# Wide attention taken apart between the first narrow heads, and two experts' products in one block

## The chip, the cores and the metric

The kernel runs on one core of a Trainium2 chip. The core has five engines, each with its own queue of instructions that it works off in order: TensorE (matrix products, PE in the profile; PEld is its loading of weights), VectorE (DVE), ScalarE (ACT), GpSimd (POOL) and SyncE (SP, which here only issues DMAs). They wait for one another by semaphores. The metric is the device time of the whole program in microseconds (us). The kernel before took 855.35 us, the median of 3 runs (854.04 to 857.73).

## The reference

The input x is 8 sequences (batches) of 512 tokens of width 128. Two layers follow, each between layer norms and with a residual:

```python
x = x + layernorm(attention(layernorm(x)))      # one head of width 128, rotary, causal
x = x + layernorm(ffn_layer(layernorm(x)))
```

`attention` is one causal head: q, k, v are products of x with 128x128 matrices, q and k are turned by rotary angles, then softmax(q k) v and an output product.

`ffn_layer` works on the same tokens, here as 8 batches of 512:

```python
h = rmsnorm(x, g1); c = h @ w_down                      # 128 -> 64
q, k, v = rope(c @ wq), rope(c @ wk), c @ wv            # 16 heads of width 4
x = x + (softmax(causal(q k / 2)) v) @ w_up             # 64 -> 128
t = rmsnorm(x, g2); probs = softmax(t @ router_w)       # 8 experts
gate = the two largest probs, divided by their sum, 0 elsewhere
y = sum over e of gate[e] * ((silu(t @ w1[e]) * (t @ w3[e])) @ w2[e])   # 128 -> 256 -> 128
return x + y
```

All experts are worked out for all tokens, and the gate is 0 for six of the eight.

## The kernel before, in words

Tokens lie on the 128 partitions, four tiles (NT = 4) of 128 tokens a batch. The first layer is called the wide attention, the 16 heads of width 4 the narrow heads.

*The wide attention* is a generator, `wide_attention`. Its loop runs over b from 0 to 9: in one turn of the loop it projects and scores batch b, turns and weighs the probabilities of batch b-1, and adds up batch b-2. `project` multiplies a product in PSUM by the rotary table into `two` (VectorE) and adds the halves (GpSimd). `scores` makes two PSUM tiles of scores; for each of the four row tiles VectorE takes the negated maximum and ScalarE the exponential. `turn_probs` turns a row tile of probabilities on TensorE (a product with the identity) and copies it to SBUF. `weigh` multiplies by the values and scales by the sums. `norm_result`, `add_result`, `add` and `norm_sum` do the layer norm of the result, the residual, and the scales `h_scale` for what follows. A `yield` is a point at which other work can be put between.

*A narrow unit* is one of 32: batch u.b, group u.g of four heads. For each unit `rowwise` makes scores by rows (tiles `sm`) of which VectorE takes the maxima into `nm` (`highest`, line 608); `lower` splits these on GpSimd in three bfloat16 parts, `turn_m` turns them (`m3T`) and SyncE puts them by DMA as further rows under q; then `columnwise` makes the same scores by columns (`sT`), less the maximum, ScalarE takes the exponential into `pk` (`weights`, line 672), and `weigh` (line 679) multiplies by the values into `po`.

`ffn_front(b)` makes q, k and v of a batch's narrow heads: four scaled tiles `hs` on GpSimd, their turn `hT`, the products `pqk` and `pvs`, the rotary part, the split in three, and six DMAs of GpSimd's queue that store q and k to DRAM (line 545). `load_rows(b)` brings them back by four DMAs, also of GpSimd's queue (line 553), as the rows that the units read. `ffn_back(b)` divides by the sums, turns (`onT`), makes `pu`, the norm, `tT` and the router's logits; `route` works out the gates of two batches at a time and puts them on the list `ready`.

*The experts.* `hidden_pieces` makes one piece at a time: two products of 128x512 (`ph`, line 851) into one wide PSUM tile, the silu on ScalarE (line 859) and a product on VectorE (line 860). Two pieces make an expert's hidden layer. `answer` makes an expert's sixteen second products (`py`, line 875), and VectorE adds them to `h_all` with the gate (line 884).

*The order.* It is written out by hand: `manual_schedule` keeps the instructions of each engine in the order in which the program issues them. `period(n)` issues the columns of unit n, the rows of unit n+2 and the last weighing of unit n-1; at its yields, `aside` puts in a step of a front, a back or a later task. Periods -2 and -1 have rows only. Before, they are issued between the last loops of the wide attention, and periods 0 to 32 follow. From the first batches with gates on, a period also has two experts: four pieces at its end with the scores of row tiles 1 and 0 between them, and the two `answer` calls of the expert pair before, spread over the row part of the next period.

*The buffers.* A pool called wide has three PSUM tiles of two banks, in turn for `sm`, `sT`, `ph`, `py`, `pqk`, `sc` and `pq`. A pool called bank has two tiles of one bank while the wide attention runs, and afterwards one, beside one for `po`. SBUF tiles `pk` have five buffers, hidden tiles four.

Of the kernel before, what the change touches and what calls it, by code (L numbers as in the profile page):

```python
# [22 lines left out]
def kernel(  # L23
# [181 lines left out]
    h_all = keep.tile([P, B * NT, D], F32, name="h_all")  # L205
    tT_all = keep.tile([P, B, T], F32, name="tT_all")
    gate_all = keep.tile([P, B * NT, E], F32, name="gate_all")
# [63 lines left out]
    def stats_x(batches):  # L271
        st = ln_stats(x_all, batches[0] * NT, "x", len(batches) * NT)
        for i, b in enumerate(batches):
            x_stats[b] = st[0][:, i * NT : (i + 1) * NT, :], st[1][:, i * NT : (i + 1) * NT]

    class Wide:
# [7 lines left out]
        def norm(self):  # L284
            b = self.b
            mv, rstd = x_stats.pop(b)
            shift = minus_product(mv[:, :, 0], rstd, "shift_x", f"shift_x_{b}")
# [15 lines left out]
        def project(self, i):  # L303
            b = self.b
            pq = wide(f"pq_{b}_{i}")
            for s in range(2):
                nc.tensor.matmul(pq[:, s, :], wqk[:, i, s, :], self.xnT, start=True, stop=True)
            two = deep.tile([P, 2, T], F32, tag="pk", name=f"two_{b}_{i}", bufs=5)
            nc.vector.tensor_tensor(two, pq, ropea, ALU.mult)
            r = work.tile([P, T], F32, tag=f"roped{i}", name=f"roped_{b}_{i}", bufs=1)  # L310
            nc.gpsimd.tensor_tensor(r, two[:, 0, :], two[:, 1, :], ALU.add)
            self.roped.append(r)
# [39 lines left out]

        def turn_probs(self, t):
            b = self.b
            n, at = (t + 1) * P, t * (t + 1) // 2 * P
            if t == 0:
                self.pT = work.tile([P, 10 * P], F32, tag="pT", name=f"pT_{b}", bufs=1)
            ps = bank(f"pT_ps_{b}_{t}")
            for j in range(t + 1):
                nc.tensor.transpose(  # L360
                    ps[:, j * P : (j + 1) * P], self.probs[t][:, j * P : (j + 1) * P], ident
                )
            if t < 2:
                nc.vector.tensor_copy(self.pT[:, at : at + n], ps[:, :n])
            else:
                nc.scalar.copy(self.pT[:, at : at + n], ps[:, :n])

# [364 lines left out]
    def normed(b):  # L732
# [23 lines left out]
        ps = transposed(ts, f"tT_ps_{b}")  # L756
        nc.scalar.activation(tT_all[:, b, :], ps, AF.Copy, scale=g2c)
        yield
        pl = bank(f"pl_{b}")
        for t in range(NT):  # L760
            nc.tensor.matmul(
                pl[:, t * E : (t + 1) * E],
                tT_all[:, b, t * P : (t + 1) * P],
                wr,
# [76 lines left out]
    def hidden_pieces():  # L841
        while True:
# [3 lines left out]
            for e in range(E):  # L846
                hid = []
                for c in range(FC):
                    ph = wide(f"ph_{b}_{e}_{c}")
                    for i, w in enumerate((w1s, w3s)):  # L850
                        nc.tensor.matmul(  # L851
                            ph[:, i, :],
                            w[:, e, c * P : (c + 1) * P],
                            tT_all[:, b, :],
                            start=True,
# [70 lines left out]

    turns, partly = [0], []
    N = B * NG
    units = [Unit(n) for n in range(N)]

    def period(n):
# [25 lines left out]
        if nxt:  # L957
            nxt.turn_m()
        answer()
        yield  # L960
# [44 lines left out]
    def wide_attention():  # L1005
# [6 lines left out]
        for b in range(B + 2):  # L1012
            yield b
            u = batches[b] if b < B else None
            nxt = batches[b + 1] if b + 1 < B else None
            v = batches[b - 1] if 0 <= b - 1 < B else None
            w = batches[b - 2] if 0 <= b - 2 < B else None
            if nxt:
                nxt.norm()
            if w:  # L1020
                w.norm_result()
            if u:
                u.project(0)
            if v:
                v.turn_probs(0)
                v.turn_probs(1)
            if u:
                u.project(1)
            yield b
            if v:  # L1030
                v.turn_probs(2)
                v.turn_probs(3)
            if w:
                w.add_result()
                w.add()
            if u:
                u.values()
            if w:
                w.norm_sum()
            yield b  # L1040
# [9 lines left out]
            if u:  # L1050
                u.scores(1)
            yield b

    def front_and_rows(b):
# [3 lines left out]

    with tc.manual_schedule():
        steps = wide_attention()  # L1060
        setup = [prepare(), fill()]
        first = [front_and_rows(0)]
        then = [period(-2), period(-1)]
        fronts.append(front_and_rows(1))
        banks(ctx, wide=3)
        with ExitStack() as stage:
            banks(stage, bank=2)
            for b in steps:
                if b > B:
                    break  # L1070
                if b < 3:
                    step(setup)
                elif b < 6:
                    step(first)
                elif b < 7:
                    step(fronts)
                else:
                    step(fronts)
                    step(then)
            while step(then):  # L1080
                step(fronts)
# [83 lines left out]
```

## Time and profile before

| what | value |
|---|---|
| median of 3 runs | 855.35 us |
| profiled execution, whole | 860.74 us |
| its span, first to last instruction | 859.0 us |
| mean granted clock of TensorE | 0.954 |
| busy: TensorE, VectorE, ScalarE, GpSimd | 761.6, 482.8, 385.2, 310.6 us |
| projections (`pq`) of batches 3 to 7 begin at | 54.1, 73.4, 85.8, 107.2, 125.1 us |
| first scores by row (`sm`) | 124.0 us |
| first product of an expert (`ph`) | about 303 us |
| copies of `m3T`, one a period, in periods 12 and 30 | 292.8 and 670.9 us |

The profile is of one execution. Its page gives the busy time of each engine over the span, 40 equal slices of the span with the busy share in tenths, groups of instructions by line, and what ended the idle time before them. "Granted clock" is the share of TensorE's full clock. A line of a timeline reads: start, length, engine, source line, operation, output<-inputs, shape, how many in a row, and in brackets the idle time before it with what ended it. A line of the windows reads: stretch, length, then busy time (number of instructions) of PE, PEld, DVE, ACT and POOL, the granted clock, the DMA share and GB/s.

### The profile page before, as it was taken

What the parts mean: (1) busy time and instruction counts of PE and PEld (TensorE: products, weight loads), DVE (VectorE), ACT (ScalarE), POOL (GpSimd) and SP (SyncE); (2) the same over time, 40 slices, a digit from 0 to 9 for tenths busy, and PEclk for the clock granted to TensorE, in tenths of its full rate; (3) what the DMA queues carried; (4) which work ended last, traced back from release to release, by engine and by line L of the source; (5) the groups of instructions that cost most, each with busy time, mean ns of one, the idle gap of its engine ahead of it and who ended that gap; (6) DMA issues with size and microseconds to landing.
All of it is one profiled execution on the core that took longest, in us unless ns stands there. A gap on an engine that the chain in (4) does not pass through costs nothing. (4 is left out here: it accounts for less than half of the span.)

```text
span 859.0 us, 15100 instructions
## 1 busy us (share of the span) xinstructions
PE 761.6 (89%) x5886; PEld 437.1 (51%) x5886; DVE 482.8 (56%) x1111; ACT 385.2 (45%) x574; POOL 310.6 (36%) x637
## 2 busy tenths in 40 slices
PE   3988687499998899999999999999999988889995
PEld 1555445244544455555545555555555555466663
DVE  2565565648566855556675655567565334364554
ACT  2464343247555644554455454554454652222221
POOL 5575868526465740425042513240114104010001
PEclk9999798559899999999999999999999999999998
DMA  9000121204022400220012002200000000000000
GB/s 281 14 6 0 56 56 56 57 2 106 11 68 48 105 10 2 56 57 14 2 57 56 14 2 56 58 14 2 2 1 14 1 2 12 1 0 13 1 13 13
DMA packets 24131, 28.74 MB, mean 33 GB/s; under 512 B 6332, under 2 KB 19292, under 8 KB 24060
## 3 DMA queue, kind: packets, MB, share of 16 engines
q0 software_dynamic: 6944, 19.03, 8.6%
q1 hardware_dynamic: 15820, 7.84, 3.3%
q8 instruction: 46, 0.75, 0.4%
q10 hardware_dynamic: 1296, 0.92, 0.4%
q14 instruction: 25, 0.20, 0.1%
HBM read 15.73 MB, written 11.53 MB: 32 GB/s over the span
## 5 line engine op out<-in xcount | busy, mean ns | idle before, releaser
L672 ACT ACTIVATE pk<-sT 128x1024 f32<-128x1024 f32 x160 | 161.9, 1024 | 113.9 <-PE sT L576 113.1
L608 DVE TENSOR_REDUCE nm<-sm 128x2 f32<-128x1024 f32 (+2 forms) x192 | 195.4, 1041 | 25.8 <-PE sm L576 23.4
L860 DVE TENSOR_TENSOR hid<-hid,ph 128x512 f32<-128x512 f32 x128 | 87.7, 686 | 155.8 <-ACT hid L859 155.2
L859 ACT ACTIVATE hid<-ph 128x512 f32<-128x512 f32 x128 | 76.0, 597 | 210.0 <-PE ph L851 172.4
L851 PE MATMUL ph<-tT_all,w1s 128*128 128x512 f32 x256 | 139.0, 625 | 6.2 <-DVE hid L860 6.2
L875 PE MATMUL py<-w2s,hid 128*128 128x128 f32 x1024 | 128.6, 279 | 4.2 <-DVE nm L608 1.3
L851 PE MATMUL ph<-tT_all,w3s 128*128 128x512 f32 x256 | 131.6, 596 | 0.0
L875 PEld LDWEIGHTS py<-w2s,hid 128*128 128x128 f32 x1024 | 120.7, 192 | 21.1 <-issue 9.8
L884 DVE SCALAR_TENSOR_TENSOR h_all<-py,gate_all,h_all 128x128 f32<-128x128 f32 x256 | 72.0, 343 | 63.8 <-PE py L875 63.7
L679 PE MATMUL po<-pk,vpad 128*32 128x512 f32 (+3 forms) x1024 | 99.2, 463 | 0.0
L217 POOL TENSOR_TENSOR root_o<-ve_o,half 128x4 f32<-128x4 f32 x8 | 8.3, 1037 | 220.6 <-DVE ve_o L234 220.6
L593 PE MATMUL sm<-k_rows,q_rows 36*128 36x256 bf16 (+3 forms) x512 | 72.2, 317 | 9.7 <-DVE nm L608 6.6
L851 PEld LDWEIGHTS ph<-tT_all,w3s 128*128 128x128 f32 x256 | 49.0, 192 | 62.1 <-issue 62.1
L593 PEld LDWEIGHTS <-q_rows 36*128 36x128 bf16 x512 | 23.5, 95 | 97.6 <-issue 94.0
L649 PE MATMUL sT<-q_rows,k_rows 39*128 39x384 bf16 (+3 forms) x512 | 64.8, 310 | 9.3 <-ACT pk L672 4.3
L431 POOL CAST m<-nm 128x16 bf16<-128x16 f32 x32 | 6.4, 199 | 176.6 <-DVE nm L608 176.1
L851 PEld LDWEIGHTS ph<-tT_all,w1s 128*128 128x128 f32 x256 | 42.4, 191 | 50.4 <-issue 17.7
L576 PE MATMUL sm<-ident_bf,mask_q 64*128 64x64 bf16 (+1 forms) x768 | 49.6, 205 | 0.0
L576 PEld LDWEIGHTS <-mask_q 64*128 64x128 bf16 x768 | 39.5, 100 | 13.6 <-issue 2.1
L576 PE MATMUL sT<-ident_bf,mask_k 64*128 64x128 bf16 (+1 forms) x640 | 43.2, 210 | 0.0
L576 PEld LDWEIGHTS <-mask_k 64*128 64x128 bf16 x640 | 31.0, 98 | 13.5 <-issue 2.0
L649 PEld LDWEIGHTS <-k_rows 39*128 39x128 bf16 x512 | 23.2, 96 | 23.1 <-issue 20.3
(170 smaller groups left out, 942.0 us busy)
## 6 DMA issues: line engine op xcount, KB each, us to landing
q_dram<-thirds POOLq DMA_DIRECT2D x24, 192.0 KB, 3.1
k_dram<-thirds POOLq DMA_DIRECT2D x24, 192.0 KB, 3.6
q_rows<-q_dram POOLq DMA_DIRECT2D x16, 288.0 KB, 5.3
k_rows<-k_dram POOLq DMA_DIRECT2D x16, 288.0 KB, 6.4
q_rows<-m3T SPq DMA_DIRECT2D x192, 2.0 KB
x_all<-in_L_attn_x_dram SPq DMA_DIRECT2D x8, 256.0 KB
out_dram<-y SPq DMA_DIRECT2D x8, 256.0 KB
w1s<-in_L_ffn_w_dram SPq DMA_DIRECT2D x2, 512.0 KB
```

Of the source, the lines that this page charges most:

```text
L217: nc.gpsimd.tensor_tensor(y, x, half[:, :n], ALU.pow)
L576: nc.tensor.matmul(out[:, :, h * HR : (h + 1) * HR], which[at, h, :], ident_bf[at, at].unsqueeze(1).to_broadcast([HR, out.shape[1], HR]), ...
L593: nc.tensor.matmul(sc[:, i, c * n : (c + 1) * n], self.q[at, 2 * self.g + pair, t * P : n], self.k[at, 2 * self.g + pair, :n], start=(c == 0),
L608: nc.vector.tensor_reduce(self.nm[:, :, pairs[0] : pairs[0] + w, t], sc[:, :, : w * n].rearrange("p i (c n) -> p i c n", n=n), AX.X, ALU.m ...
L649: nc.tensor.matmul(sc[:, i, c : c + n], self.k[at, 2 * self.g + pair, j * P : (j + 1) * P], self.q[at, 2 * self.g + pair, j * P :], start= ...
L672: nc.scalar.activation(p[:, :, :c], sc[:, :, :c], AF.Exp, scale=HD**-0.5)
L679: nc.tensor.matmul(po[h * HP : (h + 1) * HP, j * P :], vpads[self.g][:, j, h, :], self.p[j, h // 2][:, h % 2, :], start=(self.g == 0 and j ...
L851: nc.tensor.matmul(ph[:, i, :], w[:, e, c * P : (c + 1) * P], tT_all[:, b, :], start=True, stop=True,)
L859: nc.scalar.activation(hid[c], ph[:, 0, :], AF.Silu)
L860: nc.vector.tensor_tensor(hid[c], hid[c], ph[:, 1, :], ALU.mult)
L875: nc.tensor.matmul(py[:, t * P : (t + 1) * P], hid[c][:, t * P : (t + 1) * P], w2s[:, e, c, :], start=(c == 0), stop=(c == FC - 1),)
L884: nc.vector.scalar_tensor_tensor(h_all[:, n, :], py[:, t * P : (t + 1) * P], gate_all[:, n, e : e + 1], h_all[:, n, :], ALU.mult, ALU.add,)
```

## The change

It has two parts. In the first, the wide attention's loop is cut into seven pieces a turn instead of five, in a new order, and only its first five turns run alone: as soon as batch 0's narrow rows have been asked for, the periods begin, and the rest of the loop is issued piece by piece at their yields (at each in periods -2 and -1, at every second later). A period that needs a later batch's sum first issues the pieces up to it. The pool bank has one tile from period -2 on. Three row tiles of probabilities are turned together into a wide tile, and all copies of them are ScalarE's; `two` has one buffer of its own; the shift of x is worked out with its statistics; `tT` has six tiles instead of one for each batch.

In the second, a period with experts ends with one block: the rows of tiles 1 and 0, both `answer` calls of the period before, and then the four pieces. The row part has no `answer` any more.

```diff
     def stats_x(batches):
...
-            x_stats[b] = st[0][:, i * NT : (i + 1) * NT, :], st[1][:, i * NT : (i + 1) * NT]
+            rstd = st[1][:, i * NT : (i + 1) * NT]
+            mean = st[0][:, i * NT : (i + 1) * NT, 0]
+            x_stats[b] = minus_product(mean, rstd, "shift_x", f"shift_x_{b}"), rstd
...
-            two = deep.tile([P, 2, T], F32, tag="pk", name=f"two_{b}_{i}", bufs=5)
+            two = work.tile([P, 2, T], F32, tag="two", name=f"two_{b}_{i}", bufs=1)
...
-        def turn_probs(self, t):
+        def turn_probs(self, *tiles):
...
+            parts = [(t, j) for t in tiles for j in range(t + 1)]
+            n, at = len(parts) * P, tiles[0] * (tiles[0] + 1) // 2 * P
+            if len(parts) > 4:
+                ps = wide(f"pT_ps_{b}_{tiles[0]}").rearrange("p a n -> p (a n)")
+            else:
+                ps = bank(f"pT_ps_{b}_{tiles[0]}")
...
-            if t < 2:
-                nc.vector.tensor_copy(self.pT[:, at : at + n], ps[:, :n])
-            else:
-                nc.scalar.copy(self.pT[:, at : at + n], ps[:, :n])
+            nc.scalar.copy(self.pT[:, at : at + n], ps[:, :n])
...
-        nc.scalar.activation(tT_all[:, b, :], ps, AF.Copy, scale=g2c)
+        tT = tTs[b] = work.tile([P, T], F32, tag="tT", name=f"tT_{b}", bufs=6)
+        nc.scalar.activation(tT, ps, AF.Copy, scale=g2c)
...
         if u and u.g == 1 and u.b + 2 < B:
+            while u.b + 2 not in done:
+                next(wides)
             fronts.append(ffn_front(u.b + 2))
...
         if nxt:
             nxt.turn_m()
-        answer()
         yield
...
         both(2, C, u, ((0, 1),))
-        answer()
-        yield
-        mixed = bool(ready) or bool(partly)
-        if mixed:
+        yield
+        if (ready or answers) and B - 1 in done:
...
+            both(1, AC, None, None)
+            both(0, AC, None, None)
+            if v:
+                v.lower()
+                v.values()
+            answer()
+            answer()
             for i in range(2 * FC):
-                partly[:] = [b for b in (next(hidden),) if b is not None]
-                if i < 2:
-                    both(1 - i, AC, None, None)
-                if i == 2 and v:
-                    v.lower()
-                    v.values()
+                next(hidden)
                 step(later)
...
         for b in range(B + 2):
...
+            if u:
+                u.project(0)
+            if w:
+                w.norm_result()
+            yield b
+            if v:
+                v.turn_probs(0, 1, 2)
+            yield b
+            if u:
+                u.project(1)
+            if w:
+                w.add_result()
+            yield b
+            if v:
+                v.turn_probs(3)
+            if w:
+                w.add()
             if nxt:
                 nxt.norm()
...
             yield b
             if u:
                 u.values()
+            yield b
             if w:
                 w.norm_sum()
-            yield b
             if v:
                 v.weigh()
-            if b + 2 < B:
-                stats_x([b + 2])
+            yield b
             if nxt:
                 nxt.turn()
...
                 u.scores(1)
+            if b + 2 < B:
+                stats_x([b + 2])
             yield b
+            done.append(b - 2)
...
+    with tc.manual_schedule(), ExitStack() as stage:
+        banks(stage, bank=2)
+        for b in wides:
+            if b < 3:
+                step(setup)
+            else:
+                step(first) or step(fronts)
+            if b == 5 and not first:
+                break
     banks(ctx, bank=1, po=1)
     with tc.manual_schedule():
-        for n in range(N + 1):
-            for _ in period(n):
-                next(steps, None)
+        for n in range(-2, N + 1):
+            for i, _ in enumerate(period(n)):
+                if n < 0 or i % 2:
+                    next(wides, None)
                 aside()
         while ready or answers or fronts or backs or later:
-            if next(hidden) is not None:
+            more = next(hidden)
+            if more is not None:
                 aside()
                 next(hidden)
-            if len(answers) > 1 or not ready:
+            if len(answers) > 1 or more is None:
                 answer()
             aside()
```

More of the change, by code (lines that the diff above doesn't have):

```diff
@@ L205 @@
     h_all = keep.tile([P, B * NT, D], F32, name="h_all")
-    tT_all = keep.tile([P, B, T], F32, name="tT_all")
+    tTs = {}
     gate_all = keep.tile([P, B * NT, E], F32, name="gate_all")
@@ L285, in norm @@
             b = self.b
-            mv, rstd = x_stats.pop(b)
-            shift = minus_product(mv[:, :, 0], rstd, "shift_x", f"shift_x_{b}")
+            shift, rstd = x_stats.pop(b)
             self.xn = work.tile([P, NT, D], F32, tag="xn", name=f"xn_{b}")
@@ L351, in scores @@
                 self.probs.append(p)
-        def turn_probs(self, t):
+        def turn_probs(self, *tiles):
             b = self.b
-            n, at = (t + 1) * P, t * (t + 1) // 2 * P
-            if t == 0:
+            if 0 in tiles:
                 self.pT = work.tile([P, 10 * P], F32, tag="pT", name=f"pT_{b}", bufs=1)
-            ps = bank(f"pT_ps_{b}_{t}")
-            for j in range(t + 1):
+            parts = [(t, j) for t in tiles for j in range(t + 1)]
[4 more added lines that the diff above has]
+                ps = bank(f"pT_ps_{b}_{tiles[0]}")
+            for i, (t, j) in enumerate(parts):
                 nc.tensor.transpose(
-                    ps[:, j * P : (j + 1) * P], self.probs[t][:, j * P : (j + 1) * P], ident
+                    ps[:, i * P : (i + 1) * P], self.probs[t][:, j * P : (j + 1) * P], ident
                 )
-            if t < 2:
-                nc.vector.tensor_copy(self.pT[:, at : at + n], ps[:, :n])
-            else:
-                nc.scalar.copy(self.pT[:, at : at + n], ps[:, :n])
+            nc.scalar.copy(self.pT[:, at : at + n], ps[:, :n])
         def weigh(self):
@@ L762, in normed @@
                 pl[:, t * E : (t + 1) * E],
-                tT_all[:, b, t * P : (t + 1) * P],
+                tT[:, t * P : (t + 1) * P],
                 wr,
@@ L853, in hidden_pieces @@
                             w[:, e, c * P : (c + 1) * P],
-                            tT_all[:, b, :],
+                            tTs[b],
                             start=True,
@@ L925, in aside @@
         step(a) or step(b) or step(later)
-    turns, partly = [0], []
+    turns, done = [0], []
     N = B * NG
@@ L1017, in wide_attention @@
             w = batches[b - 2] if 0 <= b - 2 < B else None
+            if u:
[15 more added lines that the diff above has]
+                w.add()
             if nxt:
                 nxt.norm()
[L1020 to L1028, printed above, removed]
-            yield b
[L1030 to L1035, printed above, removed]
+            yield b
             if u:
                 u.values()
+            yield b
             if w:
                 w.norm_sum()
-            yield b
             if v:
                 v.weigh()
-            if b + 2 < B:
-                stats_x([b + 2])
+            yield b
             if nxt:
@@ L1057, in front_and_rows @@
         load_rows(b)
[L1059 to L1081, printed above, removed]
+    wides = wide_attention()
+    setup = [prepare(), fill()]
+    first = [front_and_rows(0)]
+    fronts.append(front_and_rows(1))
+    banks(ctx, wide=3)
+    with tc.manual_schedule(), ExitStack() as stage:
[7 more added lines that the diff above has]
+                break
     banks(ctx, bank=1, po=1)
     with tc.manual_schedule():
-        for n in range(N + 1):
-            for _ in period(n):
-                next(steps, None)
+        for n in range(-2, N + 1):
+            for i, _ in enumerate(period(n)):
+                if n < 0 or i % 2:
+                    next(wides, None)
                 aside()
         while ready or answers or fronts or backs or later:
-            if next(hidden) is not None:
+            more = next(hidden)
+            if more is not None:
                 aside()
                 next(hidden)
-            if len(answers) > 1 or not ready:
+            if len(answers) > 1 or more is None:
                 answer()
```

## The prediction

> **What bounds the kernel now.** I read the 40 slices first, then the windows, then the timeline.
>
> ```profile
> PE   3988687499998899999999999999999988889995
> PEclk9999798559899999999999999999999999999998
> ```
>
> A slice is 21.5 us. TensorE is the bound from slice 9 on, nearly full and at full clock. The loose stretch is slices 2 to 8 (the wide attention, then the first narrow heads): gaps, and a clock down to half. Windows (us; busy per engine; granted clock):
>
> ```profile
> 152.00:165.00 13.00, 4.59 (x50) 2.59 (x49) 11.36 (x29) 0.26 (x1) 7.73 (x17) 0.62 0.38 92
> 172.00:180.00 8.00, 7.75 (x68) 2.71 (x65) 3.66 (x4) 3.25 (x4) 3.02 (x11) 0.50 0.01 2
> 180.00:189.20 9.20, 8.94 (x71) 4.89 (x68) 3.98 (x5) 4.71 (x6) 1.01 (x5) 0.50 0.01 1
> ...
> 525.60:544.43 18.83, 18.47 (x160) 9.91 (x159) 10.73 (x19) 10.11 (x14) 5.02 (x13) 1.00 0.22 65
> 194.49:202.16 7.67, 7.10 (x111) 3.41 (x109) 6.10 (x7) 5.31 (x6) 6.63 (x14) 1.00 0.52 145
> ```
>
> From 152 to 165 VectorE's reductions (11.36 of 13) hold TensorE at 4.59. Next to last is a period with two experts: only 0.36 of 18.83 us idle. Last is one without: 0.57 of 7.67.
>
> **Part 1: wide batches in pieces.** The instruction counts hardly change: TensorE, ScalarE the same, VectorE 16 fewer (copies of turned probabilities, 345 ns each, 5.5 us, hidden: VectorE is 56% busy). So all turns on order. Batches 0 and 1 should stay (batch 2's projection starts at 41.6). From batch 2 to 4 the wide attention still runs alone, in a new order: VectorE does batch 2's statistics for the batch two back after the first rotary product, and ScalarE's four scalings (1.65) stand before the second copy of probabilities. One such batch, from its projection: reductions and exponentials of the batch before to 2.1, statistics of x 1.4, rotary product 1.2 (4.7), statistics 1.4 and `ve` (6.3), root 1.04 and shift 0.46 (7.8), scalings 1.65 (9.5), copy 0.6 (10.1), the ten weighting products 2.3, four turns 0.5, scores 2.6: 15.6, where 41.6 to 54.1 was 12.5. Batch 3, with the narrow front, by the same sum 21 (now 19.3).
>
> Batch 4 is where a DMA is moved. On GpSimd's queue:
>
> ```profile
> 94.99 0.63 POOL L545 DMA_DIRECT2D k_dram<-thirds  x1
> 100.32 1.27 POOL L407 TENSOR_TENSOR x_all<-x_all,h_all 128x512 f32<-128x512 f32 x1
> 105.98 1.49 POOL L553 DMA_DIRECT2D q_rows<-q_dram  x2 [0.41 <-issue]
> 107.45 1.32 POOL L553 DMA_DIRECT2D k_rows<-k_dram  x2
> ```
>
> Today the row loads are issued 10.4 us after the last store's issue; the stores land in 3.6, so nothing waits. In the new order only x_all's sum (1.27) stands between: the loads wait about 1.7 us on GpSimd. Queued behind them are batch 1's scaled rows, batch 2's `h_scale`, and the next shift; for the rows waits hT's transpose, which TensorE has before batch 5's projection. GpSimd's sum from the first rotary addition: additions 2.5, root and shift 1.5, thirds 1.8, six stores 3.9, sum 1.3, wait 1.7, four loads 2.8, rows 1.8, `h_scale` 2.3 = 19.6. It starts at 6.8 (after root_x and the first thirds), so hT comes at about 26.4, while scores end near 17.5: an 8.5 us stall. Batch 4 takes 28 for today's 12.4, and batch 5 starts at 41.6 + 15.6 + 21 + 28 = 106, today 85.8.
>
> Now the pieces pay. Periods -2 and -1 carry batches 5 and 6, each paced by the three wide PSUM buffers and the single bank rather than by TensorE (15.6 and 13.8 us of its work): following reductions (1.24, 0.93, 1.22, 0.68), rotary products 1.2 and statistics through VectorE's queue I get 19.4 and 18.2. Periods 0 to 5: TensorE work today at full clock 6.5, 10.0, 7.1, 7.1, 9.0, 7.7 = 47.4; the rest of the wide work 14.3; 1 us of gaps in each (today 0.57 to 1.66): 68. Periods 6 to 11 stay at 63.7, their half-clock stretch included.
>
> The clock. The Trainium skill ("TensorE: Matmul & The Clock Gate", Part 1) says that a busy window of about 3.4 us restores full clock. The rows disagree: from 172 to 189 TensorE is 97% busy at 0.50. By the page the 8.5 us stall costs some 2 us after it; if periods -2 and -1 stay at half as they do today (155 to 189), the cost is up to 17. I take 9: the neighbours are the same narrow products, but wide float32 ones now lie among them.
>
> Block starts at 106 + 19.4 + 18.2 + 9 + 68 + 63.7 = 284 instead of 293: **8.5 us gained**.
>
> **Part 2: first and second products in one block.** Around 541.33, the end of a block now (PE, ACT, DVE):
>
> ```profile
> 543.95 2.05 PE L875 MATMUL py<-w2s,hid 128*128 128x128 f32 x16
> 546.16 0.38 PE L649 MATMUL sT<-q_rows,k_rows 39*128 39x512 bf16 x2
> ...
> 542.21 1.28 ACT L672 ACT_TABLE_LOAD   x1 [0.17 <-PE sT L576]
> 543.51 1.02 ACT L672 ACTIVATE pk<-sT 128x1024 f32<-128x1024 f32 x1
> ...
> 542.67 2.35 DVE L608 TENSOR_REDUCE nm<-sm 128x2 f32<-128x1024 f32 x2
> ```
>
> After a block ScalarE loads its table and ends the first exponential 3.1 us later; VectorE, finishing the last product, frees its first score buffer at 2.6. TensorE's own work there lasts only 2.4, and `py` (1.98) covers the difference; the second `py` covers the next. Without them: the next scores wait 0.25 for the reduction, columns 0.3 for the exponential, then 0.2, 0.15 and 0.2 as three buffers pass between reduction (0.93) and exponential (1.02), and the first `py` 0.2 for the fourth exponential: about 1.2 of gaps for 0.36, **+0.8** in a plain period. Where a back's `onT` copy stands behind that exponential, `pu` waits 1.0 more: +1.3. Where hT is turned, m3T waits for its copy (0.83 today) and tT for m3T's: +0.7. The period with neither: +0.6. Mean 0.85. In the block itself (scores 0.8, two `py` 4.0, four `ph` 7.5) every buffer is back in time: a `ph` gives its own back 1.4 us after it ends, and the next user comes 3.8 later. Sixteen periods x 0.85 = 13.6, and three at the end without scores by row, 0.7 each: **15.7 lost**. Bounds: 0, if the gaps now seen (0.73 a period) only change place, and 24, if all 1.28 of the table load show in 19 periods.
>
> **Small edits.** One `two` buffer: the second product waits for the first addition (1.27), covered by 1.4 us of statistics; uncovered 1.3 a batch. Six tT tiles for eight: the seventh is wanted after batch 0's experts are done; were it not, the router would be late. Turned probabilities in a wide buffer: its ScalarE copy of 768 lies between the 512 one (0.59) and the exponential of 1024 (1.02); taken 0.8, counted above. The tail's order of products is the same: 0.
>
> **Sum.** -8.5 + 15.7 = +7, on the profiled execution (span 859.0, 860.7 with what lies around it, 5.4 above the median). I carry the difference to the median: 855.35 + 7 = **862**.
>
> **Rivals.**
> (a) *Pieces at TensorE's pace*, ends faster: if the GpSimd wait hides and the clock holds, from 106 there are 145 us of TensorE work and some 12 of gaps: block at 263, -30; with +15.7, 841. For it: slices 7 and 8 are that empty. Against: GpSimd is over half busy there and gates hT. It decides once the early gain passes 20.
> (b) *The block is hidden anyway*: gaps stay at 0.73 a period; -8.5 gives 847. For it: three engines with slack; against: periods without experts already idle as much without a table load.
> (c) *Half clock stays*: the stall is followed by 35 us more at 0.50, about +15, and gaps for the single bank: 880. For it: 172 to 189; against: slices 9 to 11 recover.
> (d) *It moves nothing*: the pieces only take up the gaps of one another, and so does the block: 855.
>
> **Numbers.** Forecast 0.42 (853 to 872; 0.10 of it within 0.5%, 0.32 above), (a) 0.16, (b) 0.14 (0.12 faster, 0.02 same), (c) 0.20, (d) 0.08 same. A change under 0.5% (4.3 us) can't be told from none. Faster 0.28, same 0.20, slower 0.52. The range cuts off the ends of (a) and (c): 840 to 884.
>
> **What would show it.** Right: batch 5's projection beyond 100; before it a gap of 5 us or more at hT, GpSimd in its loads; the first `ph` 5 to 15 us earlier than 303; plain periods with experts near 19.6, `sT` waiting for `pk` and `sm` for `nm`. Wrong: no gap at hT, full clock throughout 100 to 200, or periods at 18.8 or less.

## The result, and where the profile shows it

The changed kernel has a median of 892.1 us (4 runs, 884.60 to 903.87), the kernel before, beside it, one of 856.54 (4 runs, 854.04 to 857.78). Two of the changed kernel's runs, 899.36 and 903.87, are over 1.5% longer than its shortest and had a lower mean clock (0.920 and 0.915, for 0.934), so its ratio, like every ratio below, leaves such runs out: the other two, at 884.6 and 884.8, are **1.033 times as long** as the kernel before, 95% interval 1.029 to 1.038. The forecast was 862, its range 840 to 884.

The profile of the changed kernel is of the execution of 903.87 us. In it 154 us of the span are at half clock, in each of the two shorter executions about 117, and of those there is no trace. What it shows of the clock is therefore set beside the traces of the two parts run alone, further down.

The 40 slices of the changed kernel, each 22.6 us:

```profile
PE   3978686898989899999999999989998979889995
...
PEclk9988798799889998999699969979997998999998
```

Counted from 0, the clock row of before has nothing but 9s from slice 11 on, up to an 8 in the last. Now it has 6s in slices 19 and 23 and 7s in 26 and 30, three or four slices, about one batch, apart, and the PE row stands at 9 or 8 there: TensorE is working, at a lower clock. The sum over the span puts numbers to it. Idle is the span less TensorE's busy time; its busy time is split by the clock granted at that moment, and in the last column busy time at half clock counts half, which is roughly TensorE's work in microseconds of full clock.

| us, profiled execution | span | idle | busy at full clock | busy at half clock | work at full clock |
|---|---|---|---|---|---|
| before | 859.0 | 97.4 | 704.5 | 57.1 | 733 |
| changed | 902.1 | 112.3 | 654.5 | 135.3 | 722 |

So in this execution 15 us of the 43 are idle time, the work went down by 11, and 39 us come from 78 more microseconds spent busy at half clock.

By stage, in windows of the changed kernel (us; busy of TensorE, its weight loads, VectorE, ScalarE, GpSimd; clock; DMA). The first three are periods -1, 0 to 5 and 6 to 11, each from a turn of m3T to the next; the last is periods 12 to 29:

```profile
133.20:152.00 18.80, 13.73 (x93) 10.29 (x93) 11.93 (x32) 6.76 (x17) 13.78 (x24) 0.82 0.38 90
152.00:238.40 86.40, 72.56 (x776) 39.30 (x776) 54.43 (x101) 44.35 (x68) 42.25 (x90) 0.90 0.12 30
238.40:309.40 71.00, 64.14 (x725) 32.54 (x726) 46.03 (x71) 37.42 (x49) 41.34 (x86) 0.83 0.20 53
309.39:706.14 396.75, 371.86 (x2976) 212.56 (x2974) 223.48 (x435) 191.94 (x239) 114.50 (x253) 0.93 0.10 25
```

And of the kernel before, periods 6 to 11 and 12 to 29:

```profile
229.10:292.80 63.70, 58.26 (x723) 30.69 (x723) 43.31 (x58) 35.83 (x44) 36.34 (x78) 0.92 0.21 55
292.81:670.86 378.05, 362.55 (x2982) 198.00 (x2982) 221.89 (x438) 194.48 (x240) 114.84 (x253) 0.99 0.11 27
```

The same periods 12 to 29, with the same products, are 18.7 us longer at a clock of 0.93 for 0.99; idle time grew by 9.4 of that (396.75 - 371.86 against 378.05 - 362.55). Periods 6 to 11 hold no block, and of the wide attention only the last batch's sum (GpSimd, at 252.54) and its statistics (VectorE, at 257.11); they lost 7.3 us at 0.83 for 0.92. These stages are not peculiar to the long execution: in the trace of the pieces alone (span 868.5, below) periods 0 to 5 and 6 to 11 take 86.5 and 70.9 us at the same clocks. Of periods 12 to 29, the block alone (span 873.7) shows 389.7 us, with 41 at half clock for 58 here.

**What a fall of the clock looks like.** Windows of the changed kernel across the turn of m3T at 432.5, where period 18 begins:

```profile
427.40:430.80 3.40, 3.40 (x31) 1.34 (x31) 2.22 (x3) 2.09 (x4) 0.00 (x0) 1.00 0.02 5
430.80:434.06 3.26, 2.08 (x35) 1.20 (x35) 1.72 (x3) 2.21 (x4) 0.00 (x0) 1.00 0.00 0
434.06:440.00 5.94, 5.94 (x40) 3.70 (x39) 1.90 (x3) 3.20 (x4) 0.00 (x0) 0.50 0.01 2
440.00:447.72 7.72, 7.72 (x41) 3.43 (x41) 2.62 (x3) 2.83 (x4) 3.04 (x3) 0.50 0.00 0
```

Up to 430.8 TensorE is full. In the next 3.26 us it is busy for 2.08, no gap being longer than 0.83; then it is granted half for 13.7 us in which it has no gap at all. The gaps are these:

```profile
432.25 0.22 PE L629 MATMUL m3T_ps<-ident_bf,m 128*48 128x128 bf16 x1 [0.83 <-ACT hT L508]
432.82 0.66 PE L247 MATMUL tT_ps<-ident,ts 128*128 128x128 f32 x4 [0.35 <-ACT m3T L633]
```

They are the ones that the prediction priced at +0.7 us a period. In the kernel before, the corresponding windows are these, with the second products standing between the same small instructions:

```profile
413.60:417.00 3.40, 2.90 (x41) 1.52 (x41) 2.63 (x3) 3.10 (x4) 0.00 (x0) 1.00 0.02 5
417.00:420.50 3.50, 3.17 (x33) 2.62 (x33) 1.36 (x5) 1.04 (x3) 0.00 (x0) 1.00 0.01 1
```

Every stretch at half clock in the traces of this study has a length within 0.01 us of a multiple of 3.413, but for the last of a trace, which its end cuts. I laid a grid of 3.41 us through each of the fourteen traces, fixed at one of its stretches, and counted the windows at full clock by TensorE's busy time in them (those without any work left out):

| busy, of 3.41 us | windows | half clock follows |
|---|---|---|
| 0.1 to 1.5 | 79 | 68 |
| 1.5 to 2.5 | 293 | 85 |
| over 2.5 | 2777 | 1 |

### The profile page after: what moved, and what is told of

The parts are those of the page before. It is cut to its first block, busy times and chain, and to the rows that moved or that the text cites. A ratio compares the mean times of both kernels' runs of the same rounds, so it can differ in the third digit from the quotient of the medians.

```text
span 902.1 us, 15067 instructions
## 1 busy us (share of the span) xinstructions
PE 789.8 (88%) x5886; PEld 463.7 (51%) x5886; DVE 484.7 (54%) x1095; ACT 384.6 (43%) x574; POOL 311.3 (35%) x637
## 5 line engine op out<-in xcount | busy, mean ns | idle before, releaser
L855 PE MATMUL ph<-tT,w1s 128*128 128x512 f32 x256 | 132.4, 599 | 6.2 <-DVE hid L864 6.2
L855 PE MATMUL ph<-tT,w3s 128*128 128x512 f32 x256 | 131.6, 596 | 0.0
L879 PEld LDWEIGHTS py<-w2s,hid 128*128 128x128 f32 x1024 | 122.6, 196 | 16.7 <-issue 12.4
L682 PE MATMUL po<-pk,vpad 128*32 128x512 f32 (+3 forms) x1024 | 106.5, 486 | 3.8 <-ACT pk L675 3.8
L855 PEld LDWEIGHTS ph<-tT,w3s 128*128 128x128 f32 x256 | 48.9, 191 | 61.8 <-issue 61.8
L652 PE MATMUL sT<-q_rows,k_rows 39*128 39x384 bf16 (+3 forms) x512 | 67.8, 319 | 11.6 <-DVE nm L611 6.3
L596 PEld LDWEIGHTS <-q_rows 36*128 36x128 bf16 x512 | 26.0, 97 | 93.0 <-issue 88.8
L855 PEld LDWEIGHTS ph<-tT,w1s 128*128 128x128 f32 x256 | 45.6, 192 | 49.1 <-issue 30.4
L579 PE MATMUL sT<-ident_bf,mask_k 64*128 64x128 bf16 (+1 forms) x640 | 46.4, 217 | 0.0
L579 PEld LDWEIGHTS <-mask_k 64*128 64x128 bf16 x640 | 33.6, 101 | 12.9 <-issue 3.5
L308 PE MATMUL pq<-xnT,wqk 128*128 128x512 f32 x64 | 37.8, 722 | 2.1 <-ACT p L345 1.6
```

Source lines behind the costliest of these rows:

```text
L579: nc.tensor.matmul(out[:, :, h * HR : (h + 1) * HR], which[at, h, :], ident_bf[at, at].unsqueeze(1).to_broadcast([HR, out.shape[1], HR]), ...
L596: nc.tensor.matmul(sc[:, i, c * n : (c + 1) * n], self.q[at, 2 * self.g + pair, t * P : n], self.k[at, 2 * self.g + pair, :n], start=(c == 0),
L652: nc.tensor.matmul(sc[:, i, c : c + n], self.k[at, 2 * self.g + pair, j * P : (j + 1) * P], self.q[at, 2 * self.g + pair, j * P :], start= ...
L682: nc.tensor.matmul(po[h * HP : (h + 1) * HP, j * P :], vpads[self.g][:, j, h, :], self.p[j, h // 2][:, h % 2, :], start=(self.g == 0 and j ...
L855: nc.tensor.matmul(ph[:, i, :], w[:, e, c * P : (c + 1) * P], tTs[b], start=True, stop=True,)
L879: nc.tensor.matmul(py[:, t * P : (t + 1) * P], hid[c][:, t * P : (t + 1) * P], w2s[:, e, c, :], start=(c == 0), stop=(c == FC - 1),)
```

## The experiments

The runs fall into three sittings, each on a chip of its own. The kernel before, run in all three, has medians of 859.59 us (20 runs), 854.62 (23) and 857.98 (27). A ratio is to the kernel before in the same sitting; times of different sittings can differ by the 5 us that these do. The first sitting has the block alone, the pieces alone, `block_filled` and `pieces_sync`; the second `block_gap_filled`, `half_block`, `pieces_copy_first` and `pieces_mended`; the third the other four.

The time that an execution spent at half clock is 2 x (1 - mean clock) x span. Over the 70 executions of the kernel before it lies between 58 and 94 us (59 in the shortest, 849.38; 94 in the longest, 868.53), with a slope of 0.44 us of time per microsecond at half clock. The first two runs take the change apart.

**The block alone.** Part 2 of the change, on the kernel before:

```diff
         if nxt:
             nxt.turn_m()
-        answer()
         yield
...
         both(2, C, u, ((0, 1),))
-        answer()
         yield
-        mixed = bool(ready) or bool(partly)
-        if mixed:
+        if ready or answers:
...
+            both(1, AC, None, None)
+            both(0, AC, None, None)
+            if v:
+                v.lower()
+                v.values()
+            answer()
+            answer()
             for i in range(2 * FC):
```

> Only the second part of the change: the block of both second products and the four pieces, the wide attention as before. The changed kernel's profile shows half-clock stretches of 7 to 14 us in its periods with experts that the kernel before has not, each behind a stretch of about 3.4 us in which TensorE was busy for 2.3 us or less. Theory G (the clock): the block has taken the second products out of the thin stretch where hT, m3T and tT wait for their copies, so half clock comes there and costs the time: 866 to 880, with half-clock stretches near the m3T of the third group of each batch, and plain periods at 18.7, no longer than before. Theory W (my prediction's: waits for buffers): 871, but with every period with experts 0.6 to 1.3 longer at full clock, and the clock as before.

876.95 us (865.91 to 880.95), ratio 1.013 (1.002 to 1.024). Half clock 115 us in the median, for 76 in the kernel before.

**The pieces alone.** Part 1, with the experts as before:

```diff
-        if (ready or answers) and B - 1 in done:
+        if (ready or partly) and B - 1 in done:
```

(and the two `answer` calls and the scores between the pieces put back).

> Only the first part of the change: the wide attention in pieces, one bank buffer from period -2 on; the second products spread over the row part as before. If the first part is a gain that the block hides (rival: pieces pay), 847 or less. If its early stretch costs what the changed kernel's profile shows (period 12 at 309 instead of 293), 868 to 873. Batch 5's projection at 105 to 109 in both.

870.33 us (869.56 to 874.76), ratio 1.012 (1.007 to 1.017). Half clock 76 us, as in the kernel before. Both parts lose, and within the intervals their ratios account for the change: 1.013 x 1.012 is 1.025, for 1.033. In microseconds of 859 these ratios are 11 for the block and 10 for the pieces; the medians differ by 17 and 11. In the same terms as above:

| us, profiled execution | span | idle | busy at full clock | busy at half clock | work at full clock |
|---|---|---|---|---|---|
| block alone | 873.7 | 110.8 | 676.6 | 86.3 | 720 |
| pieces alone | 868.5 | 100.3 | 702.9 | 65.3 | 736 |

The block brings nearly all of the change's idle time, all of its saved work, and 29 us more busy at half clock. The pieces bring 3 us idle, 3 us of work and 8 us busy at half clock, which counts half: a sum of small things, +9.5. The two do not add up to the 78 us of the change, whose profiled execution is a long one; the time at half clock over the executions does so more nearly (+39 and +1, for some +45 in the changed kernel's two shorter ones).

**Does the clock cost the time, or only accompany it?** Two periods in the trace of the block alone answer for themselves. Periods 14 and 22 have the same instructions on TensorE:

```profile
327.93:350.88 22.95, 22.41 (x187) 13.19 (x188) 11.84 (x20) 11.28 (x15) 9.60 (x16) 1.00 0.19 53
492.98:522.09 29.11, 28.57 (x187) 15.97 (x188) 11.82 (x20) 11.28 (x14) 9.58 (x16) 0.77 0.15 42
```

The idle time is 0.54 us in both. Period 22 has a stretch of 13.65 us at half clock and is 6.16 longer: 0.45 us for each. The kernel before takes 23.33 for either. So where TensorE is full, half clock costs the time.

What brings it was tried by filling. The block alone, with TensorE given products that nobody reads, so that it works more. First, 8 ahead of the second pairs' tile-3 scores in the third group's periods (the place of the windows above):

```diff
-        both(3, C, None, None)
+        both(3, C, None, None, 8 if u and u.g == 2 and (ready or answers) else 0)
...
+            for _ in range(fill):
+                nc.tensor.matmul(
+                    sc[:, 0, :P], wqk[:, 0, 0, :], wqk[:, 0, 1, :], start=True, stop=True
+                )
```

> The block alone, with eight more products of 128x128 (float32, about 1.0 us together) put into the thin stretch of the four periods with experts that have a front or its place: they are written to the score tile ahead of the real scores and overwritten. Work is only added. Theory G: these periods keep full clock and fall from 29 to about 24, so it is faster than the block alone by 4 x 4 to 5 less what does not show, some 10 to 18. Theory W: slower than the block alone by up to 4.

875.62 us (872.34 to 876.06), ratio 1.016 (1.011 to 1.021). A miss: the time hardly moved. The condition holds in periods 14, 18, 22 and 26. The first three ran at full clock (22.95 us), but in the profile of the block alone only one of them had not (22, with 29.11); in 26 a stretch of 3.4 us went. The period ahead of each grew by 0.9 (ahead of 26 by 1.6), and the stretches of 10.2 us in periods 25 and 29 stayed. It settles nothing.

Then 20 ahead of tT's turns in periods 25 and 29. The block alone there (a window and the first line of what follows):

```profile
562.71:566.12 3.41, 1.55 (x28) 0.76 (x20) 1.60 (x2) 2.93 (x3) 2.79 (x8) 1.00 0.01 2
566.12:576.36 10.24, 9.04 (x51) 5.50 (x52) 2.88 (x7) 3.25 (x4) 2.44 (x5) 0.50 0.09 28
```

```profile
566.98 0.47 PE L247 MATMUL tT_ps<-ident,ts 128*128 128x128 f32 x1 [2.71 <-POOL ts L750]
```

TensorE waits 2.71 us for `ts`, which GpSimd makes, where formerly second products lay.

```diff
-        ps = transposed(ts, f"tT_ps_{b}")
+        ps = transposed(ts, f"tT_ps_{b}", fill=20 if b in (5, 6) else 0)
```

> The block alone, with 20 products of 128x128 (float32, about 2.5 us together) ahead of the four turns of tT in two periods (25 and 29), where the block alone shows a gap of 2.7 us at tT (GpSimd is late with its input) and 10.2 us at half clock behind it. They write to the same PSUM tile and are overwritten. Work is only added, mostly into the gap. Theory G (a thin stretch of some 3.4 us brings half clock): no half clock behind the two gaps, periods 25 and 29 fall from 27.4 to about 22 to 23, the time is 8 to 10 less than the block alone's at the same clock elsewhere. Theory W: 0 to 3 more.

```profile
559.32 3.95 PE L247 MATMUL tT_ps<-wqk 128*128 128x128 f32 x33
```

```profile
557.80:561.20 3.40, 3.40 (x44) 2.64 (x37) 1.64 (x2) 2.96 (x3) 2.75 (x9) 1.00 0.01 2
561.20:564.60 3.40, 3.40 (x34) 3.17 (x34) 0.00 (x0) 0.08 (x1) 2.50 (x5) 1.00 0.29 83
564.60:575.00 10.40, 10.06 (x80) 7.01 (x77) 5.93 (x18) 3.66 (x5) 1.02 (x5) 1.00 0.00 0
```

The 20 products take 4.73 us, not the 2.5 expected. Yet periods 25 and 29 take 24.63 and 24.47 us instead of 27.39 and 27.35, without half clock: **products that nobody needs make each of the two periods 2.8 or 2.9 us shorter.** In these periods nothing else differs, so there the thin stretch brought half clock, and half clock cost the time.

Of the whole time this does not show. It is 864.04 us (858.42 to 872.58), 13 below the block alone's 876.95, but in another sitting, and the ratios, 1.011 (1.004 to 1.017) for 1.013 (1.002 to 1.024), can't be told apart. In the two traces 6.2 us of the difference are period 22's, which was not filled: the stretch of 13.65 us did not come there this time. Half clock is 76 us in the median, for 66 in the kernel before; in the block alone it was 115 for 76.

**Half a block.** One second product in the row part, behind m3T's turn, one in the block:

```diff
         if nxt:
             nxt.turn_m()
         answer()
         yield
...
         both(2, C, u, ((0, 1),))
-        answer()
         yield
...
+            both(1, AC, None, None)
+            both(0, AC, None, None)
...
+            answer()
             for i in range(2 * FC):
```

> The wide attention as before; of the two second products one stays in the row part (behind m3T, where the kernel before has its first), the other goes into the block. Theory G: the product in the row part keeps the thin stretches full, so the clock is as before (half-clock total near 75 us), and what the block saves at full clock (0.1 to 0.9 a period) shows: 848 to 856. Theory W: half of the prediction's loss, 858 to 866.

856.11 us (852.87 to 862.72, 20 runs), ratio 1.0013 (0.9988 to 1.0039): the time does not differ from before. Half clock is 82 us, for 66 in the kernel before. With one second product left among the row part's small ones, less clock is lost than with none (16 us above the kernel before, for 39).

**The same, with the first group's second product later.** In first-group periods the row part's `answer` stands where the second one of the kernel before stands, to keep TensorE busy where `ts` comes late:

```diff
-        answer()
+        if not v or n % NG != 1:
+            answer()
...
-        answer()
+        if not v or n % NG == 1:
+            answer()
...
-            answer()
+            if v:
+                answer()
```

> One second product in the block, as in the half block, but in the periods that hold an expert's transposes of hT and ts (the first group's) the other one stands behind the tile-2 scores, where the kernel before has its second; the last two periods keep both in the row part. Clock theory: the half-clock stretches behind 560, 646 and 700 us go, the total comes back to 66 to 70 us, and the time is 848 to 853. Rival (those stretches only fall on other periods, or the saving was never the clock's): 856, as the half block.

857.89 us (853.76 to 865.20, 22 runs), ratio 1.0006 (0.9982 to 1.0031), half clock 83 us for 72. The clock theory's numbers are missed. In the traces, of the half block's three stretches of 6.8 us the one in period 25 is still there (at 567.9), the one in period 29 is half as long (3.4 at 653.3), and the last is gone: the gaps at tT in period 25, behind `ts`, fell only from 1.7 to 1.4 us. I could mend the clock in a place by filling, but not foresee it from an order.

**The waits of the early part.** In the changed kernel TensorE's longest gaps before batch 5's projection are these, and the pieces alone have the same within 0.4 us:

```profile
52.86 4.64 PE L376 MATMUL pr<-v,pT 128*128 128x128 f32 x20 [4.03 <-ACT pT L369]
69.60 1.77 PE L247 MATMUL hT_ps<-ident,hs 128*128 128x128 f32 x4 [3.15 <-POOL hs L445]
94.41 4.63 PE L376 MATMUL pr<-v,pT 128*128 128x128 f32 x20 [5.62 <-ACT pT L369]
104.52 0.76 PE L247 MATMUL hT_ps<-ident,hs 128*128 128x128 f32 x2 [2.17 <-POOL hs L445]
107.81 0.91 PE L247 MATMUL hT_ps<-ident,hs 128*128 128x128 f32 x2 [2.54 <-POOL hs L445]
```

Three runs tried to take them out of the pieces alone. Batch 0's row loads on SyncE's queue:

```diff
-                nc.gpsimd.dma_start(out=rows[i * HR : i * HR + S9], in_=halves[i])
+                queue.dma_start(out=rows[i * HR : i * HR + S9], in_=halves[i])
```

> The pieces alone, with the first loads of rows (batch 0's four DMAs) on SyncE's queue instead of GpSimd's. If these loads in GpSimd's queue are what holds hT (4.7 us of gaps ahead of batch 5's projection in the changed kernel), the gaps shrink to 1 or less, batch 5's projection comes 4 to 6 earlier and the time is 4 to 8 less than with the pieces alone. If the scaled rows are late for another reason (the sums and scales ahead of them), the gap stays over 3 and the time within 2.

867.29 us (863.58 to 876.07, 17 runs), ratio 1.012 (1.008 to 1.016), as for the pieces alone. The gap of 2.54 is gone, the one before it stays at 2.25: the loads behind the stores are a small part of the stall.

ScalarE's last copy of turned probabilities ahead of the sum of the result:

```diff
             if u:
                 u.project(1)
-            if w:
-                w.add_result()
             yield b
             if v:
                 v.turn_probs(3)
             if w:
+                w.add_result()
                 w.add()
```

> The pieces alone, with the last row tile's turn and its copy put ahead of the four scalings of add_result on ScalarE (they wait for GpSimd's shift). If this order is the cause of the gaps of 4.0 and 5.6 us at pr, both go, batch 5's projection comes at 95 to 98 instead of 105 and the time falls by 7 to 12 from the pieces alone. If pr waits for something else by then (the copy of v, or the sums), the time falls by 3 or less.

877.16 us (871.31 to 877.45), ratio 1.026 (1.020 to 1.032) for the pieces' 1.012: slower, and so a miss. The gap at `pr` did not go, it moved one instruction on:

```profile
92.33 0.90 PE L247 MATMUL xnT_ps<-ident,xn 128*128 128x128 f32 x3 [4.88 <-ACT v L326]
```

ScalarE, not the copy's place, is late. And both together, with `norm_result` ahead of the first projection:

```diff
-            if u:
-                u.project(0)
             if w:
                 w.norm_result()
+            if u:
+                u.project(0)
```

> As pieces_copy_first, and besides norm_result ahead of the first projection (as in the kernel before) and the first loads of rows on SyncE's queue. If the wide order's waits are the whole loss of the first part, batch 5's projection comes at 90 to 94, and with what the pieces win back later (7 us) the time is 848 to 856. If half clock or the single bank takes it back later, 858 to 866.

874.34 us (870.20 to 877.57), ratio 1.025 (1.019 to 1.030). Batch 5's projection begins at 98.5 instead of 104.8, so the early part did gain 6 us, but the turn of m3T in period 12 is at 306.2 for 305.0: periods 6 to 11 spent 34 us at half clock instead of 24. What the waits gave, later stages took back.

**Can filling win outright?** The kernel before with unread products, 128 in all, in periods -2 to 10 (its clock is half there for 51 us, in three stretches from 144.9 on). Their operands are float32, not bf16 as the expectation says:

```diff
-                v.rowwise(t, pairs)
+                v.rowwise(t, pairs, 6 if n < 0 else 0)
...
+            if n in (-1, 0):
+                warm(16)
+            elif n in (2, 6, 10):
+                warm(8)
```

> The kernel before with products that nobody reads (bf16, 128 columns): 6 ahead of each row tile's scores in periods -2 and -1, 16 ahead of m3T's turns in periods -1 and 0, 8 ahead of them in periods 2, 6 and 10. Clock theory: the half-clock stretches from 145 to 189 and 230 to 240 us shrink, 842 to 850. Rival (added work is paid for, the clock there depends on something else): 856 to 862.

868.17 us (863.26 to 872.01), ratio 1.011 (1.006 to 1.017), half clock 50 us for 72. The clock came, the time did not: the products took 32.5 us of TensorE. Windows of this kernel over periods -1 and 6 to 11:

```profile
159.60:171.80 12.20, 12.14 (x123) 10.74 (x125) 7.32 (x15) 0.26 (x1) 3.58 (x10) 1.00 0.43 98
234.90:295.30 60.40, 55.59 (x738) 30.45 (x739) 43.39 (x59) 35.81 (x45) 36.26 (x78) 1.00 0.22 59
```

Period -1 is now at full clock and busy throughout, and takes 12.20 us for the 12.40 of before, when it was at 0.59, TensorE busy for 4.00 and VectorE for 10.99. So there it was VectorE that set the length, and half clock can have cost little; that it cost nothing is not shown, since the added products now fill the period by themselves. Periods 6 to 11 gained 3.3; the turn of m3T ahead of all this is 6.8 us later for the products added.

The late half block with the same filling:

> The late half block and the unread products of the kernel before with them, together. Clock theory: both savings add, 838 to 848. Rival: 853 to 860.

866.99 us (862.90 to 871.48, 6 runs), ratio 1.012: the same loss.

The changed kernel with both fillings of the block:

> The changed kernel with both sets of unread products: 8 ahead of the second pairs' tile-3 scores in the third group's periods with experts, 20 ahead of tT's turns in periods 25 and 29. They add some 8 to 10 us of work. Clock theory: the half clock of periods 14, 18, 22, 25 and 29 (51 us in the profiled execution) goes, and the time falls by 10 to 20, to 872 to 882. Rival (the clock is not what made the change slow): 892 plus the work added, 898 to 902.

889.43 us (879.65 to 891.50), ratio 1.034 (1.028 to 1.040), for 1.033 without the filling: a miss, nothing was gained. The added products take 17.4 us, not 8 to 10. Where they stand, most of the half clock went; periods 12 to 29 of this kernel:

```profile
313.27:696.12 382.85, 366.22 (x3120) 218.65 (x3119) 224.51 (x438) 191.89 (x240) 114.55 (x253) 0.99 0.11 27
```

That is 13.9 us shorter than 396.75, at 0.99 for 0.93, though the 396.75 are of the long execution. In this profile, periods 6 to 11, well ahead of any filling and with the same code, took 75.0 us for 71.0, with 37.5 us at half clock for 23.9. So the stages are no independent terms. That the place of the grid of windows on the program decides part of it is likely, but not shown. No version tried beats the kernel before.

## Why the prediction was wrong, step by step

By size it is part 1 that failed. The forecast had -8.5 us for it and +15.7 for the block; run alone, part 1 costs 10 or 11 us, and the block 11 by its ratio and 17 by the medians. The block's number came out near for another reason than the one given, and that is luck, as the steps below show.

**Batch 5's projection at 106: near, in part by luck.** It is at 108.5 in the profile. Batches 2, 3 and 4 take 18.5, 21.5 and 26.1 us for the 15.6, 21 and 28 of the sum, so its misses partly cancel. The wait at hT behind GpSimd is 2.17 and 2.54, where I had put 8.5; 4.03 and 5.62 stand earlier, at `pr`, behind ScalarE's copy, which the sum did not have. Rival (a) fell with it; slice 8, which it counts as empty, is 9 tenths busy, at half clock.

**Periods -2 and -1: right in the sum.** 106 + 19.4 + 18.2 + 9 for the clock put the turn of m3T in period 0 at 152.6; it is at 152.1. From batch 5's projection on, 43.6 us stand for 46.6, with 13.7 us at half clock on the way (two stretches of 6.8, at 106.4 and 140.5), which can have cost 7 at most and not 9.

**"Periods 0 to 5 ... 68": wrong, 86.4.** This step failed first. It had 61.7 of work at full clock and 6 us of gaps; measured are 13.8 us idle, and 72.6 busy, of which 15.6 at half clock. So 8 us more are idle, 8 went to the clock, which this step put at nothing, and 3 are more work. Two of the gaps, in the timeline of the changed kernel:

```profile
157.10 0.34 PE L596 MATMUL sm<-k_rows,q_rows 36*128 36x384 bf16 x2 [2.34 <-ACT p L345]
165.29 1.54 PE L366 MATMUL pT_ps<-ident,p 128*128 128x128 f32 x6 [1.42 <-DVE nm L611]
```

The wide batch's scores hold a wide PSUM buffer until ScalarE's exponential, and the narrow scores behind them wait: the pieces take gaps up and make others. That was the content of rival (d), which I had given 0.08.

**"Periods 6 to 11 stay at 63.7, their half-clock stretch included": wrong, 70.9.** Idle 6.8 for 5.4, half clock 23.9 for 10.2. I carried the clock over with the code, as though it were a property of those instructions. The two steps miss by 18.4 and 7.2 us, which is the difference between 284 and the measured 309.4 for the turn of m3T in period 12: a gain of 8.5 became a loss of 16.6 (12.2 in the pieces alone, where that turn is at 305.0). The first `ph` is at 317.3, not 5 to 15 us earlier than 303.

**The block's gaps: right in kind, in size by luck.** Sixteen periods at +0.85 and three at 0.7 made 15.7. The idle time of periods 12 to 29 rose by 9.4 and that of the tail, all behind period 30's turn of m3T, by 3.0: 12.4 in all, but mostly not where the sum had them. 6.0 of the 9.4 are the wait of tT for `ts`, behind GpSimd, in two periods (2.71 at 566.98 above), which the sum did not have. The `m3T` gaps for hT's copy were there before (2.5 us in all, and 2.5 now). In a plain period:

```profile
373.12:391.82 18.70, 17.93 (x157) 10.23 (x157) 10.91 (x19) 10.00 (x13) 3.13 (x9) 1.00 0.03 7
```

0.77 us idle for the 0.36 of before, +0.4 where the forecast had +0.8, with `sT` behind `pk` and behind `nm`:

```profile
373.27 0.47 PE L652 MATMUL sT<-q_rows,k_rows 39*128 39x512 bf16 x2 [0.24 <-ACT pk L675]
...
375.77 0.40 PE L652 MATMUL sT<-q_rows,k_rows 39*128 39x384 bf16 x4 [0.28 <-DVE nm L611]
```

**"A plain period 19.6": wrong, 18.70.** The sum took TensorE's own work as unchanged. It fell from 18.47 to 17.93: a block of like products is shorter than the same products with scores between them. In the block each `ph` product (two records in the trace) takes 0.86 from start to start:

```profile
381.76 1.02 PE L855 MATMUL ph<-tT,w1s 128*128 128x512 f32 x2
382.62 1.02 PE L855 MATMUL ph<-tT,w3s 128*128 128x512 f32 x2
```

and in the kernel before 0.96 where a product stands next to a change between float32 and bf16:

```profile
533.09 1.12 PE L851 MATMUL ph<-tT_all,w1s 128*128 128x512 f32 x2
534.05 1.02 PE L851 MATMUL ph<-tT_all,w3s 128*128 128x512 f32 x2
535.01 0.39 PE L593 MATMUL sm<-k_rows,q_rows 36*128 36x256 bf16 x4
```

Over a period the `ph` take 6.97 for 7.47 and the `py` 3.68 for 3.98. So at full clock the block's gaps are paid back, by a saving and not by cover. An estimate from the traces of the block alone and of before, with half of the time busy at half clock taken off: periods 12 to 29 take 370.6 us for 374.6, the tail 190.2 for 186.4. The outcome would have been near the zero that rival (b) had for the block.

**The clock of the block phase: the step that is missing.** The prediction looked at the clock only in the early part. It priced each gap of the block by its length, and put the clock there at nothing. What these gaps did, with the second products gone from between the small ones, was to leave a window of 3.41 us thin, and 3.4 to 13.7 us of dense work behind it then ran at half. Of the 28 us between the changed kernel's two shorter executions and before, the half clock (117 us for 72) is worth some 20 at 0.44 us each; of the block alone's 11 to 17 us, the half clock (115 us for 76) is worth some 17, that is, all. Both are estimates, with the slope of the kernel before. The Trainium skill, "TensorE: Matmul & The Clock Gate", Part 1, which I weighed for how full clock comes back, has it lost after an idle window of about 3.4 us; in the windows at 432.5 it was lost after gaps no longer than 0.83 us, TensorE being busy for 2.08 of 3.26 us. The measurement decides. The same page's "A second HAM failure mode: psum-queue depth-cycling" tells of a clock that swings when TensorE pauses often and briefly between groups of products. This case is of that kind, and the section could have warned of it, though it gives no share or length from which to work out a loss.

**Rival (c)**, half clock at about 880, came nearest, for another place: I had it behind the early stall, not in the block.

**Open.** How many windows a stretch at half clock lasts (one to ten here) I could not derive, nor why 85 of 293 windows busy for 1.5 to 2.5 us are followed by one and the others not; the busy share is a condition, not the whole rule. In the changed kernel filling brought no gain, so what it would take at full clock throughout no run shows. That part 1's loss is the sum given above is read from its trace; no run isolates its terms.

## What to carry to other kernels

Before gathering dense work of a tightly filled engine into one block, look at what is left between the blocks: by the table above, windows of about 3.4 us in which TensorE is busy for less than some 2.5 are where its clock may fall, and then the dense block pays, at twice the time. Read the clock row beside the busy row for each stage, and price a gap by the work that stands behind it, not by its length. Where TensorE waits for another engine anyway, half clock can cost little, so look at that engine first.

## What had not been expected of the hardware

- Half clock came in stretches of 3.4 to 34 us, multiples of 3.41, after one sparse window; a gap of 0.83 us, with a smaller one, was enough. 13.7 us of gapless work followed at 0.50 before full clock came back.
- Between executions of one kernel the time at half clock differs (58 to 94 us before), and with it the time, by 0.44 us for each; most of the spread of 849 to 869 us goes with it. The same period took 22.95 us at full clock and 29.11 with 13.65 us at half.
- 20 added float32 products of 128 columns (4.73 us) ahead of a wait of 2.71 us made each of two periods 2.8 or 2.9 us shorter.
- A float32 product of 512 columns took 0.96 us where a bf16 product stood before or behind it, and 0.86 between float32 products. What of the change makes the difference was not tried.
